# Selective scan in the last layer of a four-layer image network: which engine adds softplus' parts and multiplies by B, and where layer norm's PSUM tiles come from

## The chip, the cores and the metric

The kernel runs on one core of a Trainium2 chip. The time is the device time of one execution in microseconds (us). The core's engines are TensorE (PE, matmuls, with weight loads shown apart as PEld), VectorE (DVE), ScalarE (ACT), GpSimd (POOL), and SyncE (SP), which here issues nearly all transfers. Each engine works through its own queue in order; semaphores tie the queues together.

## The reference

Four layers follow each other on an image of 2 x 128 channels x 64 x 64: attention, a convolution block with deformable branches, three steps of a residual convolution, and a layer of selective scans. The change touches the last one alone. For each of two images it normalises over the channels, then runs the same scan block ("mamba") over the 4096 pixels in four orders (rows, rows backwards, columns, columns backwards), joins the four outputs by a linear layer and adds the input:

```python
xh, z = jnp.split(x @ W_in.T, 2, axis=-1)          # 256 channels each
xh = silu(causal_conv4(xh) + conv_b)
x_dbl = xh @ W_xp.T                                # 8 + 16 + 16 columns: dt, B, C
dt = softplus(x_dbl[..., :8] @ W_dt.T + b_dt)
dA = jnp.exp(dt[..., None] * -jnp.exp(A_log))      # decays, 256 x 16 states
dBu = dt[..., None] * Bm[:, :, None, :] * xh[..., None]
h = dA_t * h + dBu_t                               # over the pixels
y = jnp.einsum('lbdn,bln->bld', hs, Cm) + xh * Dp
return (y * silu(z)) @ W_out.T
```

## The kernel before

`layer3` cuts the work into 64 blocks: two images x four orders x eight stretches of 512 pixels (`BLK`). A block has 256 channels x 16 states = 4096 recurrences, which lie on 128 partitions as eight groups: two halves `hf` of the channels x four `ng` of the states. In a group, partition 32 j + c holds state 4 ng + j of channel c of a quarter, and the four quarters `q` lie beside each other: a tile `db` of 128 x 4 x 512. I call one of these 128 x 512 parts a state-column; a block has 32.

What is done for a group, and on which engine:

- `weights` (L1370, PE): a matmul with a selecting matrix spreads the four rows of B over the partitions, into the PSUM tile `pbc` (pool `psb`, two buffers).
- `db_dve` (L1386, DVE): `pbc` times dt x u for the first n of the four state-columns, n from the table `ND[hf][ng]`.
- `db_pool` (L1395, POOL): the other 4 - n state-columns, from a copy of B in SBUF. `copies` (L1380) brings these copies, and those of C, with four transfers each, for the groups that need them.
- `expo` (L1402, ACT): the decay of one state-column, into a PSUM tile `da` (pool `psd`, three buffers); it is issued two state-columns ahead.
- `scan` (L1411, DVE): the recurrence of one state-column, in place in `db`.
- `keep` (L1416, ACT): the last column of the four, for the next block.
- `cmul` (L1421, POOL): `db` times C for all four.
- `sums` (L1429, PE): four matmuls that sum over the states into `py` (one buffer); with the first `ng` also L1427, the product of u and D.
- `gate` (L1438, DVE): `py` times silu(z), once per half.

The tiles `db` come from a pool of four buffers, so a group's product waits for the sums of the group four before it.

What a block needs before its scans, its front, is spread over the eight turns of the loop (`slot`) of the block before: convolution (`begin`, `conv`, L1284), `conv_silu` (L1289), `xproj` and `xproj_copy` (L1308, L1314, L1316), `delta` (L1334), `softplus` (L1340 to L1343), `xproj_rest` (L1326, L1327) with `rest_copy` (L1330), which make the low part of B and C, `zproj` with `zproj_silu` (L1296, L1302), `spread` (L1348, L1349, POOL), and `spread_store`, `spread_load`, `bc_store` on SP, which lay dt and dt x u out on the partitions by way of DRAM. All front tiles in PSUM come from one pool, `psm`, with two buffers. Softplus is made from two parts, relu(v) in `dd[:, 0]` and ln(1 + exp(-|v|)) in `dd[:, 1]`.

What a block needs after its scans: `project` (L1446, L1448, PE: the image itself through an identity matrix, plus the output matmuls) and `finish` (L1454, L1456 or L1459, ACT), in slots 3 and 4 of the block after.

The layer norm of the first image runs ahead of the scans; that of the second (`ln_mean`, `ln_square`, `ln_var`, `ln_scale`, `ln_store`, L1211 to L1242) runs beside eight late blocks of the first image.

The order on every engine is the order in which the loop issues (`tc.manual_schedule`). A turn of the loop issues, in this order: transfers, `weights(k + 2)`, four times `expo` and `scan` with `keep(k - 1)` after the first expo, the products of group k + 1, `cmul(k - 1)`, the front's matmuls, the front's work on ACT and POOL, `project` or `finish`, the layer norm's step, and `sums(k - 2)`.

Of the kernel before, what the change touches and what calls it, by code (L numbers as in the profile page):

```python
# [20 lines left out]
P = 128  # L21
NB = 2
# [30 lines left out]
def interior(g, b, r0=0, rows=HW):  # L53
    return g.xa[:, b, 1 + r0 : 1 + r0 + rows, 1 : 1 + HW]
# [7 lines left out]
def img(t):  # L62
    return t.rearrange("p (r w) -> p r w", w=HW)
# [1057 lines left out]
def layer3(g, I, out):  # L1121
# [5 lines left out]
    nc, tc = g.nc, g.tc  # L1127
    NJ = 4

    ND = ((2, 4, 2, 4), (2, 4, 1, 4))  # L1130
    NNG = N_STATE // NJ
    HB = 1
    HC = 3
    with ExitStack() as ctx:
# [6 lines left out]

        winz = a.tile([P, 2, P], F32, name="winz")
        nc.sync.dma_start(winz, I["winzT"])
        wxp = a.tile([P, 2, 40], F32, name="wxp")
        nc.sync.dma_start(wxp, I["wxpT"])
        wdt = a.tile([40, 2, P], F32, name="wdt")
        nc.sync.dma_start(wdt[32:40], I["wdtT"])
        am = a.tile([P, 2, 4, NNG], F32, name="am")
        nc.sync.dma_start(am, I["alog4"])
        onesm = a.tile([P, P], F32, name="onesm")  # L1150
# [55 lines left out]
        N = {}  # L1206


        def ln_mean(b, k):
            N[k, "mean"] = psm.tile([P, BLK], F32, name="pm3")  # L1210
            nc.tensor.matmul(N[k, "mean"], onesm, interior(g, b, k * RB, RB), start=True, stop=True)  # L1211

        def ln_square(b, k):
            if b == 0:

                t = wk.tile([P, 4, BLK], F32, name="db")
                N[k, "xc"], N[k, "sq"] = t[:, 0, :], t[:, 1, :]
            else:
                N[k, "xc"] = ck.tile([P, BLK], F32, name="xc", bufs=1)
                N[k, "sq"] = ck.tile([P, BLK], F32, name="sq", bufs=1)  # L1220
            xc = N[k, "xc"]
            nc.vector.tensor_sub(img(xc), interior(g, b, k * RB, RB), img(N[k, "mean"]))  # L1222
            nc.scalar.activation(N[k, "sq"], xc, AF.Square)

        def ln_var(b, k):
            N[k, "var"] = psm.tile([P, BLK], F32, name="pm3")
            nc.tensor.matmul(N[k, "var"], onesm, N[k, "sq"], start=True, stop=True)

        def ln_scale(b, k):

            nc.scalar.activation(N[k, "sq"], N[k, "var"], AF.Ln, bias=g.eps5)
            nc.scalar.activation(N[k, "sq"], N[k, "sq"], AF.Exp, scale=-0.5)
            nc.gpsimd.tensor_mul(N[k, "xc"], N[k, "xc"], N[k, "sq"])

        def by_row(k):
# [69 lines left out]
        def xproj(i):  # L1305
            S[i]["px"] = px = psm.tile([P, BLK], F32, name="pm3")
            for hf in range(2):
                nc.tensor.matmul(px[:40, :], wxp[:, hf, :], S[i]["u"][:, hf, :], start=(hf == 0), stop=(hf == 1))  # L1308

        def xproj_copy(i):  # L1310

            px = S[i].pop("px")
            S[i]["xd"] = ck.tile([40, BLK], F32, name="xd", bufs=1)
            nc.scalar.copy(S[i]["xd"], px[:40, :])  # L1314
            bc = S[i]["bc"] = ck.tile([4 * N_STATE, BLK], F32R, name="bc")
            nc.scalar.copy(bc[0:32], px[0:32, :])  # L1316

# [13 lines left out]

        def delta(i, hf):
            pdt = S[i]["pdt", hf] = psm.tile([P, BLK], F32, name="pm3")
            nc.tensor.matmul(pdt, wdt[32:40, hf, :], S[i]["xd"][32:40], start=True, stop=True)  # L1334

        def softplus(i, hf):

# [4 lines left out]
            nc.scalar.activation(dd[:, 1, :], dd[:, 1, :], AF.Exp, scale=-1.0)  # L1342
            nc.scalar.activation(dd[:, 1, :], dd[:, 1, :], AF.Ln, bias=g.one)  # L1343

        def spread(i, hf):
            s_ = S[i]
            dd = s_["dd", hf]
            nc.gpsimd.tensor_add(dd[:, 0, :], dd[:, 0, :], dd[:, 1, :])  # L1348
            nc.gpsimd.tensor_mul(dd[:, 1, :], dd[:, 0, :], s_["u"][:, hf, :])  # L1349

        def spread_store(i, hf):
# [98 lines left out]
        def finish(i):  # L1450
            b, nd, c = blocks[i]
            s_ = S.pop(i)
            if nd == 0:
                nc.scalar.activation(s_["xv"], img(s_["pf"]), AF.Identity, bias=vec(g, "b_fuse"))  # L1454
            elif nd < 3:
                nc.scalar.copy(s_["xv"], img(s_["pf"]))  # L1456
            else:
                res = ck.tile([P, BLK], F32, name="sq", bufs=1)
                nc.scalar.copy(res, s_["pf"])  # L1459
                nc.sync.dma_start(out[b, :, c * BLK : (c + 1) * BLK], res)  # L1460

# [10 lines left out]
        def front_act(i, slot):  # L1472
            if i < NBK:
                if slot == 0:
                    conv_silu(i)
                elif slot == 1:
                    xproj_copy(i)
                elif slot == 2:
                    softplus(i, 0)
                elif slot == 3:  # L1480
                    softplus(i, 1)
                elif slot == 4:
                    rest_copy(i)
                elif slot == 5:
                    zproj_silu(i)


        def transfers(i, slot):
            if i < NBK:
                if slot == 2:  # L1490
                    bc_store(i)
                elif slot == 4:
                    spread_store(i, 0)
                elif slot == 5:
                    spread_load(i, 0)
                    spread_store(i, 1)
            if slot == 0 and i - 1 < NBK:
                spread_load(i - 1, 1)
            for x, ahead in (("b", 3), ("c", 1)):
                j, ng = divmod(8 * (i - 1) + slot + ahead, 8)  # L1500
                if ng < NNG and 0 < j < NBK:
                    copies(j, x, ng)

        def front_pe(i, slot):
            if i < NBK:
                if slot == 1:
                    xproj(i)
                elif slot == 2:
                    delta(i, 0)
                elif slot == 3:  # L1510
                    delta(i, 1)
                elif slot == 4:
                    xproj_rest(i)
                elif slot == 5:
                    zproj(i)
            if i + 1 < NBK:
                if slot == 6:
                    begin(i + 1)
                elif slot == 7:
                    conv(i + 1, 1)  # L1520

        def front_pool(i, slot):
# [1 line left out]
                if slot in (3, 4):  # L1524
                    spread(i, slot - 3)

        LN = {6: ln_mean, 7: ln_square, 8: ln_var, 9: ln_scale, 10: ln_store}

        def next_norm(i, slot):

            for j, s in ((i, slot), (i - 1, slot + 8)):
                b, k = divmod(j, 4 * NBLK)
                k -= 4 * NBLK - 2 - NBLK
                if j >= 0 and b + 1 < NB and 0 <= k < NBLK and s in LN:
                    LN[s](b + 1, k)

        with tc.manual_schedule():
            tc.keep_in_program_order(nc.scalar.preload_act_table_set("natural_log_exp_and_others"))
# [7 lines left out]
            for t in range(NBLK + 2):  # L1546
# [12 lines left out]
                elif slot in (3, 4):  # L1559
                    spread_store(0, slot - 3)  # L1560
                    if slot == 3:
                        spread_load(0, 0)
                        copies(0, "b", 0)
                        copies(0, "c", 0)
                for s in LN:
                    if 0 <= t - s // 8 < NBLK:
                        LN[s](0, t - s // 8)
                if t == 1:
                    begin(0)
                    conv(0, 1)  # L1570
            for ng in range(1, NNG):
                copies(0, "b", ng)
                copies(0, "c", ng)
            units = [(k, q) for k in range(len(groups)) for q in range(4)]
            AHEAD = 2
            for u in range(AHEAD):
                expo(*units[u])
            for k in range(len(groups) + 6):
                i, slot = divmod(k, 8)
                live = k < len(groups)  # L1580
                more = k + 1 < len(groups)
# [1 line left out]
                transfers(i + 1, slot)  # L1583
                if k + 2 < len(groups):
                    weights(k + 2)
                for q in range(4):
                    if 4 * k + q + AHEAD < len(units):
                        expo(*units[4 * k + q + AHEAD])
                    if q == 0 and ended:
                        keep(k - 1)  # L1590
                    if live:
                        scan(k, q)

                    for j, hf in (((k - 6) // 8, 0), ((k - 10) // 8, 1)):
                        if q == 1 and 8 * j + 6 + 4 * hf == k and 0 <= j < NBK:
                            gate(j, hf)
                if more:
                    db_dve(k + 1)
                    db_pool(k + 1)
                if ended:  # L1600
                    cmul(k - 1)
                front_pe(i + 1, slot)
                front_act(i + 1, slot)
                front_pool(i + 1, slot)
                if i >= 1 and i <= NBK:
                    if slot == 3:
                        project(i - 1)
                    elif slot == 4:
                        finish(i - 1)
                if live:  # L1610
                    next_norm(i, slot)

                    if slot == 6 and i % (4 * NBLK) < NBLK // 2:
                        for n in range(2):
                            turn(blocks[i][0], 2 * (i % (4 * NBLK)) + n)

                if 0 <= k - 2 < len(groups):
                    sums(k - 2)


# [86 lines left out]
def _arrays(i):  # L1707
# [26 lines left out]
    for d, (n, s) in enumerate((("offx", slice(0, 9)), ("offy", slice(9, 18)))):  # L1734
# [3 lines left out]
            for j, v in enumerate(("g", "b", "beta")):  # L1738
                offv[c, j] = l1[f"{n}_{v}"][s]
    wxp = l3["W_xp"]  # L1740
    wxp = np.concatenate([wxp[DTR:], wxp[:DTR]])
    a = {
        "x": i["x"].reshape(NB, P, L),
        "vecs": np.stack([cols[n] for n in VEC], axis=1),
# [5 lines left out]
        "w1T": taps(l2["w1"]), "w2T": taps(l2["w2"]),  # L1750
        "winX": l3["W_in"][: 2 * P].reshape(2, P, P).transpose(1, 0, 2),
        "winzT": l3["W_in"][2 * P :].reshape(2, P, P).transpose(2, 0, 1),
        "wxpT": wxp.reshape(40, 2, P).transpose(2, 1, 0),
        "wdtT": l3["W_dt"].reshape(2, P, DTR).transpose(2, 0, 1),

        "alog4": l3["A_log"].reshape(2, 4, 32, 4, 4).transpose(4, 2, 0, 1, 3).reshape(P, 2, 4, 4),
# [21 lines left out]
```

## Time and profile before

| | us |
|---|---|
| median of 3 runs | 5967.48 (5966.78 to 5974.58) |
| the profiled execution | 5965.63 |
| its span, first to last instruction | 5963.8 |
| first scan | 2517.65 after the span's start |
| DVE busy | 4521.3 (76%) |
| POOL busy | 3653.1 (61%) |
| ACT busy | 3768.4 (63%) |
| PE busy | 4905.1 (82%) |

The busy shares are means over four very different layers. The scans begin at 2517.65 us and fill the rest, some 3430 us. What bounds that stretch is read from windows within it. In a group of instructions, "busy" is the time covered by at least one of them; instructions of one engine overlap a little, so that a scan of 1265 ns comes every 1.18 us.

### The profile page before, as it was taken

The numbers are of one execution on the slowest core, as the hardware profiler recorded it, in microseconds if no ns is written. First come the engines' busy times: TensorE is split into PE (matmuls) and PEld (weight loads), VectorE is DVE, ScalarE is ACT, GpSimd is POOL, SyncE is SP. The second block draws the span as 40 slices with busy tenths as digits, with TensorE's granted clock in tenths as the row PEclk, the third lists the DMA queues.
The fourth block names the chain that finished last, engine by engine and source line by source line (L and its number), as shares of the span: only waits on it lengthen the run. The fifth ranks groups of instructions, "written<-read, shape, count | busy, mean of one in ns | idle before, by whom it ended". The sixth has DMA issues, their size and how long they took to land.

```text
span 5963.8 us, 57478 instructions
## 1 busy us (share of the span) xinstructions
PE 4905.1 (82%) x18726; PEld 1661.7 (28%) x18726; DVE 4521.3 (76%) x4266; ACT 3768.4 (63%) x5371; POOL 3653.1 (61%) x1328
## 2 busy tenths in 40 slices
PE   7999999989978689877777777777777777777776
PEld 3333333334444234222222222222222222222221
DVE  5333333364134688599999999999999999999998
ACT  4888888830035411477666766767776766767665
POOL 5111111100010121299999999999999999999998
PEclk8999999999989899877778777877788777877776
DMA  5000001030066100255555555554565555555554
GB/s 153 18 18 18 19 18 33 1 58 1 15 116 113 48 4 0 52 135 123 125 126 139 135 123 124 128 134 116 136 139 131 127 122 130 139 130 126 126 136 99
DMA packets 333092, 541.85 MB, mean 91 GB/s; under 512 B 66504, under 2 KB 121168, under 8 KB 331696
## 3 DMA queue, kind: packets, MB, share of 16 engines
q1 hardware_dynamic: 329648, 534.54, 39.0%
q10 hardware_dynamic: 3136, 3.56, 0.2%
q8 instruction: 149, 2.44, 0.2%
q14 instruction: 159, 1.30, 0.1%
HBM read 448.78 MB, written 89.13 MB: 90 GB/s over the span
## 4 chain that ended last, share of the span: by engine, by line
PE 39%; DVE 37%; ACT 6%; issue 6%; DMA 6%; POOL 4%; SPq 1%; DVEq 0%; POOLq 0%; ACTq 0%
DVE db L1411 25%; PE ps L287 10%; DVE db L1386 10%; PE acc L303 8%; PE m L1052 5%; PE m L566 5%; DMA dx<-dd 3%; POOL db L1421 2%; ACT da L1402 2%; PE acd L812 2%; PE pm L1296 1%; PE m L526 1%; ACT L1303 1%; ACT L1302 1%; PE pf L775 1%
## 5 line engine op out<-in xcount | busy, mean ns | idle before, releaser
L1421 POOL TENSOR_TENSOR db<-db,c 128x2048 f32<-128x2048 f32 x512 | 2310.7, 4528 | 21.6 <-ACT hl L1416 21.1
L1411 DVE TENSOR_TENSOR_SCAN db<-da,hl,db 128x512 f32<-128x512 f32 x1792 | 2165.0, 1265 | 61.3 <-ACT da L1402 14.9
L1402 ACT ACTIVATE da<-dd,am 128x512 f32<-128x512 f32 x2048 | 1403.5, 689 | 963.3 <-DVE db L1411 953.7
L293 ACT ACTIVATE e<-ps 128x1024 f16<-128x1024 f32 x1024 | 992.2, 1021 | 134.7 <-PE ps L287 117.5
L1386 DVE TENSOR_TENSOR db<-pbc,dd 128x2048 f32<-128x2048 f32 (+2 forms) x512 | 851.8, 1664 | 19.8 <-PE py L1429 18.2
L1370 PE MATMUL pbc<-bc,sel 64*128 64x512 f32 x512 | 288.5, 564 | 571.7 <-DVE db L1386 571.4
L1395 POOL TENSOR_TENSOR db<-b,dd 128x1024 f32<-128x1024 f32 (+1 forms) x256 | 671.6, 2623 | 119.9 <-issue 94.5
L1429 PE MATMUL py<-db,fold 128*32 128x512 f32 x4096 | 640.5, 703 | 104.8 <-POOL db L1421 104.7
L314 DVE RECIPROCAL rec<-acc 32x512 f32<-32x512 f32 x64 | 214.9, 3358 | 639.2 <-PE acc L303 612.1
L321 POOL TENSOR_TENSOR parts<-parts 32x512 f32<-32x512 f32 x64 | 80.4, 1256 | 975.3 <-DVE parts L320 975.3
L287 PE MATMUL ps<-q,k 32*128 32x512 f32 x4096 | 656.2, 643 | 3.5 <-DVE flag L250 2.7
L303 PE MATMUL acc<-e,v 128*128 128x512 f16 x2048 | 531.3, 382 | 0.0
L1052 PE MATMUL m<-v,u 128*128 128x512 f32 x864 | 377.2, 600 | 51.0 <-DVE v L1021 51.0
L1370 PEld LDWEIGHTS pbc<-bc,sel 64*128 64x128 f32 x512 | 106.2, 208 | 1113.4 <-DVE db L1386 1048.3
L1284 PE MATMUL pm<-xn,wcs 128*128 128x512 f32 x512 | 285.0, 708 | 56.9 <-DVE xc L1222 46.3
L1411 DVE TENSOR_TENSOR_SCAN db<-da,db 128x512 f32<-128x512 f32 x256 | 294.4, 1205 | 17.4 <-ACT da L1402 8.7
L303 PEld LDWEIGHTS <-v 128*128 128x128 bf16 x2048 | 158.5, 97 | 509.8 <-issue 388.5
L287 PEld LDWEIGHTS ps<-q,k 32*128 32x128 f32 x4096 | 229.7, 183 | 227.9 <-issue 147.1
L1284 PE MATMUL pm<-xt,wcs 128*128 128x512 f32 x512 | 279.2, 696 | 11.3 <-ACT z L1302 11.3
L1427 PE MATMUL py<-u,ddp 128*128 128x512 f32 x256 | 186.4, 818 | 101.7 <-DVE gt L1438 101.7
L566 PE MATMUL m<-comb,w 64*128 64x512 f32 (+4 forms) x1296 | 269.9, 575 | 0.0
L686 POOL TENSOR_SCALAR yt<-y 32x512 f32<-32x512 f32 x8 | 18.2, 2270 | 381.2 <-DVE y L677 380.8
(315 smaller groups left out, 5970.5 us busy)
## 6 DMA issues: line engine op xcount, KB each, us to landing
dd<-dx SPq DMA_DIRECT2D x1024, 256.0 KB, 6.6
dx<-dd SPq DMA_DIRECT2D x128, 512.0 KB, 8.7
c<-bx SPq DMA_DIRECT2D x1024, 64.0 KB, 2.3
hats<-pos SPq DMA_DIRECT2D x136, 256.0 KB, 9.6
b<-bx SPq DMA_DIRECT2D x512, 64.0 KB, 5.2
q<-qd SPq DMA_DIRECT2D x32, 512.0 KB, 8.6
w<-in_conv0T SPq DMA_DIRECT2D x18, 288.0 KB, 8.5
q<-in_x SPq DMA_DIRECT2D x8, 512.0 KB, 7.6
```

The costliest lines, as they stand in the source:

```text
L287: nc.tensor.matmul(ps[:, i, :], k4[h % 2][rows, kb // 4, :], q4[h % 2][rows, qb * BLK : (qb + 1) * BLK], start=True, stop=True,)
L293: nc.scalar.activation(e[:, :n, :], ps[:, :n, :], AF.Exp)
L303: nc.tensor.matmul(acc, v3[b][:, kb, h, :], e[:, i, :], start=(kb == 0), stop=(kb == NS - 1))
L566: yield lambda q=q, dy=dy, src=src, i0=i0, i1=i1: nc.tensor.matmul(m[:, i0 * NF : i1 * NF], w[half, dy, q, x, :], src, start=(dy == KC and ...
L1052: nc.tensor.matmul(m[x], weights[j][:, dy, x, :], v[j][b][:, x, r0 : r0 + RP, :].rearrange("p r i -> p (r i)"), start=(dy == 0), stop=(dy ...
L1284: nc.tensor.matmul(pu, wcs[:, hf, s, :], window(blk, sgn * s), start=(s == 0), stop=(s == 3))
L1386: nc.vector.tensor_tensor(x["db"][:, :n, :], x.pop("pb").unsqueeze(1).to_broadcast([P, n, BLK]), S[i]["d4", hf][:, 1, :n, :], ALU.mult)
L1395: nc.gpsimd.tensor_tensor(x["db"][:, n:, :], S[i]["b", ng].unsqueeze(1).to_broadcast([P, 4 - n, BLK]), S[i]["d4", hf][:, 1, n:, :], ALU.mult)
L1402: nc.scalar.activation(da, S[i]["d4", hf][:, 0, q, :], AF.Exp, scale=am[:, hf, q, ng : ng + 1])
L1411: nc.vector.tensor_tensor_scan(d1, d0, d1, 0.0 if first else hl[:, hf, ng, q, :], ALU.mult, ALU.add)
L1421: nc.gpsimd.tensor_mul(v, v, S[i]["c", ng].unsqueeze(1).to_broadcast([P, 4, BLK]))
L1429: nc.tensor.matmul(S[i]["y", hf][32 * q : 32 * q + 32, :], fold, G[k]["db"][:, q, :], start=False, stop=(ng == NNG - 1),)
```

## The change

- **Products with B.** The table `ND` gives DVE 21 of a block's 32 state-columns where it had 23, and POOL 11 where it had 9, in other groups; three of the four `ng` need a copy of B in SBUF instead of two.
- **Softplus.** The two parts are added by PE: `sum_parts` multiplies both by the identity into one PSUM tile of `psm`, and `sum_copy` (ACT) writes the sum over `dd[:, 0]`. `spread` on POOL loses its addition.
- **dt.** W_xp gets a second copy of its dt rows at row 64, so that each half's `delta` reads its own eight rows; both halves' matmuls are issued in slot 1.
- **The front's slots.** The front moves one slot ahead, with `conv_silu` at the end of slot 7 of the block before; `project` goes from slot 3 to slot 5, after the sums of that slot, and `finish` from slot 4 to the head of slot 6.
- **Layer norm.** Its two PSUM tiles come from the pool of the decays. Its steps for the second image are placed by hand in slots 0, 1, 3, 4 and 6.
- `finish` has a tile of its own, `res`, for the last order's result.

The diff, cut to its core:

```diff
-    ND = ((2, 4, 2, 4), (2, 4, 1, 4))
+    ND = ((4, 2, 1, 4), (1, 4, 1, 4))
...
-        wxp = a.tile([P, 2, 40], F32, name="wxp")
+        wxp = a.tile([P, 2, 72], F32, name="wxp")
...
+        def ln_tile():
+            return psd.tile([P, BLK], F32, name="da")
         def ln_mean(b, k):
-            N[k, "mean"] = psm.tile([P, BLK], F32, name="pm3")
+            N[k, "mean"] = ln_tile()
...
         def delta(i, hf):
             pdt = S[i]["pdt", hf] = psm.tile([P, BLK], F32, name="pm3")
-            nc.tensor.matmul(pdt, wdt[32:40, hf, :], S[i]["xd"][32:40], start=True, stop=True)
+            r = slice(32 + 32 * hf, 40 + 32 * hf)
+            nc.tensor.matmul(pdt, wdt[r], S[i]["xd"][r], start=True, stop=True)
...
+        def sum_parts(i, hf):
+            ps = S[i]["dt", hf] = psm.tile([P, BLK], F32, name="pm3")
+            for x in range(2):
+                nc.tensor.matmul(ps, g.ident, S[i]["dd", hf][:, x, :], start=(x == 0), stop=(x == 1))
+        def sum_copy(i, hf):
+            nc.scalar.copy(S[i]["dd", hf][:, 0, :], S[i].pop(("dt", hf)))
         def spread(i, hf):
             s_ = S[i]
             dd = s_["dd", hf]
-            nc.gpsimd.tensor_add(dd[:, 0, :], dd[:, 0, :], dd[:, 1, :])
             nc.gpsimd.tensor_mul(dd[:, 1, :], dd[:, 0, :], s_["u"][:, hf, :])
...
         def front_act(i, slot):
             if i < NBK:
                 if slot == 0:
-                    conv_silu(i)
+                    xproj_copy(i)
                 elif slot == 1:
-                    xproj_copy(i)
+                    softplus(i, 0)
                 elif slot == 2:
-                    softplus(i, 0)
+                    softplus(i, 1)
+                    sum_copy(i, 0)
                 elif slot == 3:
-                    softplus(i, 1)
+                    sum_copy(i, 1)
+                    rest_copy(i)
                 elif slot == 4:
-                    rest_copy(i)
-                elif slot == 5:
                     zproj_silu(i)
+            if i + 1 < NBK and slot == 7:
+                conv_silu(i + 1)
...
         def front_pe(i, slot):
             if i < NBK:
-                if slot == 1:
+                if slot == 0:
                     xproj(i)
+                elif slot == 1:
+                    delta(i, 0)
+                    delta(i, 1)
                 elif slot == 2:
-                    delta(i, 0)
+                    sum_parts(i, 0)
                 elif slot == 3:
-                    delta(i, 1)
+                    sum_parts(i, 1)
+                    xproj_rest(i)
                 elif slot == 4:
-                    xproj_rest(i)
-                elif slot == 5:
                     zproj(i)
             if i + 1 < NBK:
-                if slot == 6:
+                if slot == 5:
                     begin(i + 1)
-                elif slot == 7:
+                elif slot == 6:
                     conv(i + 1, 1)
...
                 if k + 2 < len(groups):
                     weights(k + 2)
+                norm = next_norm(i)
+                if slot == 6 and 1 <= i <= NBK:
+                    finish(i - 1)
                 for q in range(4):
+                    if norm and slot == 3 and q == 3:
+                        ln_log(*norm)
                     if 4 * k + q + AHEAD < len(units):
                         expo(*units[4 * k + q + AHEAD])
+                    if norm and q == 0:
+                        if slot == 0:
+                            ln_mean(*norm)
+                        elif slot == 3:
+                            ln_var(*norm)
...
+                if norm and slot == 0:
+                    ln_less(*norm)
                 if more:
                     db_dve(k + 1)
                     db_pool(k + 1)
                 if ended:
                     cmul(k - 1)
+                if slot == 5 and 0 <= k - 2 < len(groups):
+                    sums(k - 2)
+                if slot == 5 and 1 <= i <= NBK:
+                    project(i - 1)
                 front_pe(i + 1, slot)
                 front_act(i + 1, slot)
                 front_pool(i + 1, slot)
-                if i >= 1 and i <= NBK:
-                    if slot == 3:
-                        project(i - 1)
+                if norm:
+                    if slot == 1:
+                        ln_square(*norm)
+                    elif slot == 3:
+                        ln_root(*norm)
                     elif slot == 4:
-                        finish(i - 1)
+                        ln_scale(*norm)
+                    elif slot == 6:
+                        ln_store(*norm)
...
-                if 0 <= k - 2 < len(groups):
+                if slot != 5 and 0 <= k - 2 < len(groups):
                     sums(k - 2)
```

`bc_store` moves from slot 2 to slot 1. Ahead of the loop, the first image's layer norm goes through the same new functions, and `conv_silu` of block 0 follows its convolution.

## The prediction

> **What bounds the kernel now.** I read the stages first, then the waits, then one block in order of time. The stretch from the first to the last scan lasts 3430 us of the span. Its columns are length, busy time (instructions) of PE, PEld, DVE, ACT and POOL, clock, DMA share, GB/s:
>
> ```profile
> core 0: us, PE busy (x) PEld busy (x) DVE busy (x) ACT busy (x) POOL busy (x), PEclk, DMA share, GB/s
> 2600.00:5900.00 3300.00, 2506.45 (x7100) 703.49 (x7098) 3213.14 (x2592) 2306.03 (x3732) 3165.05 (x993) 0.79 0.56 130
> ```
>
> DVE is busy 97.4% and POOL 95.9%: two engines near their end, so the waits decide. All that DVE waits for there is some 36 us; POOL waits three times as much:
>
> ```profile
> POOL db L1395 <- issue: 90.2, 53, 3.4
> ...
> DVE db L1386 <- PE py L1429: 18.2, 8, 2.9
> ...
> DVE db L1411 <- ACT da L1402: 15.6, 58, 0.5
> ```
>
> So DVE sets the pace. I number the eight groups of a block, and the loop's turns (slots), 0 to 7; T3 is the start of slot 3's first scan. DVE's timeline, from slot 3's scans to slot 7's:
>
> ```profile
> 3336.61 4.81 DVE L1411 TENSOR_TENSOR_SCAN db<-da,hl,db 128x512 f32<-128x512 f32 x4
> 3341.34 1.20 DVE L1386 TENSOR_TENSOR db<-pbc,dd 128x1024 f32<-128x1024 f32 x1
> 3342.64 4.81 DVE L1411 TENSOR_TENSOR_SCAN db<-da,hl,db 128x512 f32<-128x512 f32 x4
> 3347.36 2.26 DVE L1386 TENSOR_TENSOR db<-pbc,dd 128x2048 f32<-128x2048 f32 x1
> 3349.73 4.81 DVE L1411 TENSOR_TENSOR_SCAN db<-da,hl,db 128x512 f32<-128x512 f32 x4
> 3354.45 0.67 DVE L1386 TENSOR_TENSOR db<-pbc,dd 128x512 f32<-128x512 f32 x1
> 3355.22 2.46 DVE L1411 TENSOR_TENSOR_SCAN db<-da,hl,db 128x512 f32<-128x512 f32 x2
> 3357.60 0.67 DVE L1438 TENSOR_TENSOR gt<-py,z 128x512 f32<-128x512 f32 x1
> 3358.52 2.46 DVE L1411 TENSOR_TENSOR_SCAN db<-da,hl,db 128x512 f32<-128x512 f32 x2 [0.26 <-ACT da L1402]
> 3360.90 2.27 DVE L1386 TENSOR_TENSOR db<-pbc,dd 128x2048 f32<-128x2048 f32 x1
> 3363.27 4.81 DVE L1411 TENSOR_TENSOR_SCAN db<-da,hl,db 128x512 f32<-128x512 f32 x4
> ```
>
> From start to start, a slot lasts 6.03 us if the product at its end is two state-columns wide, 7.09 if four, 5.49 if one. A gate adds 0.59. Slot 6 lasts 8.05, not 7.68: DVE waits for a decay, 0.26 us plus lost overlap (0.35). A block is 4 x 7.09 + 3 x 6.03 + 5.49 + 2 x 0.59 + 0.35 = 53.5 us, with no room left.
>
> **What the Trainium skill says.** "GPSIMD Engine Reference", 3.1: a two-input operation on 2048 fp32 takes 4497 ns on GpSimd and 2293 on VectorE; here 4528 (L1421) and 2264 (L1386). Its section 1 says that the two share SBUF interfaces, with contention when VectorE has two SBUF inputs; here L1421 takes 4.49 to 4.56 us beside scans and products alike, each of which reads one input from PSUM. "PSUM — Partial Sum Buffer", Specifications: GpSimd has no access to PSUM, so a product moved there needs B in SBUF. "TensorE: Matmul & The Clock Gate", Part 1: the array runs at half rate until a window of about 3.4 us was busy. Agreed, and sharper: in 3.41 us intervals the clock (after the busy time) is 0.50 or 1.00.
>
> ```profile
> 3378.78:3382.19 3.41, 3.41 (x10) 0.50 0.10 22
> 3382.19:3385.61 3.42, 2.31 (x9) 1.00 0.24 78
> 3385.61:3389.02 3.41, 2.57 (x9) 0.50 0.00 0
> ...
> 3392.43:3395.85 3.42, 3.42 (x5) 0.50 0.00 0
> 3395.85:3399.26 3.41, 3.41 (x15) 1.00 0.19 76
> ```
>
> Over all such intervals from 2700 to 5900 us, at half clock about 2.65 us of matmuls bring the full clock next, and at full clock about 1.4 us keep it; the 8-row L1334 and the 64-row L1370 don't count.
>
> **The change, part by part.**
>
> *Products.* Widths on DVE by group go from 2,4,2,4,2,4,1,4 to 4,2,1,4,1,4,1,4: 21 state-columns for 23. A block of slots is then 4 x 7.09 + 6.03 + 3 x 5.49 + 2 x 0.59 = 52.04. Against 53.13 without the wait, DVE gains 1.09 us by these rounded steps; the rows' means give 2 x (1197 - 663) = 1.07. I take 1.05, and x 64 blocks **-67 us**.
>
> *POOL.* Rows:
>
> ```profile
> L1395 POOL TENSOR_TENSOR db<-b,dd 128x1024 f32<-128x1024 f32 x192 | 451.6, 2352 | 119.9 <-issue 94.5 <-DMA c<-bx 14.3 <-POOL db L1421 4.5
> ...
> L1395 POOL TENSOR_TENSOR db<-b,dd 128x1536 f32<-128x1536 f32 x64 | 220.0, 3437 | 0.0
> ...
> L1348 POOL TENSOR_TENSOR dd<-dd 128x512 f32<-128x512 f32 x128 | 162.2, 1267 | 0.0
> ```
>
> Three two-wide and one three-wide product (10.5) become one and three (12.7); both adds L1348 go (-2.5); eight L1421 (36.1) and two L1349 (2.5) stay. 51.7 becomes 51.3, starts overlapping a little: about 51.1, inside DVE's 52.0. About 1 us per block is left for waits. Now POOL loses 1.7 us a time to the sums of group 0 (90.2/53; L1395 starts at 3336.12, L1429 ended at 3335.96). After it, sum_parts stands ahead of those sums on PE; they end 6.6 to 8.3 us after T2 (below), POOL arrives at about 7.3. A wait of at most 1 us, 0.3 on average: covered.
>
> *DMA.* One more copy of B, four 64 KB transfers a block on SP (b and c copies took 8.7 us for eight at 3353). Chain: end of POOL's spread, store 2.7, loads 3.8, store 0.6, eight copies 8.7, landing 5.2 (median) = 21 us; POOL has 22.7 us of work before it needs group 1's copy. Cost 0, margin 1.6. bc_store moves ahead of c's third copy, which is needed two slots later: 0.
>
> *Softplus.* Per half two fp32 matmuls (four rows: 2.0 us at full clock, 4.0 at half, from L1446 and L1448) and one ACT copy (0.58). PE gains 4 us of 52 at full clock, ACT 1.2.
>
> *ScalarE's slots.* An expo needs a free da tile, so in each slot ACT starts its other work 4.38 us after T (3349.73 to 3354.11) and the next expo is ready 0.72 after that work; DVE wants it at the next T + 2.38, or 2.97 with a gate. Check: now slot 5 has zproj's 3.68, 4.38 + 3.68 + 0.72 = 8.78 against 5.49 + 2.97 = 8.46: the measured wait. After: slot 0 6.2 against 8.4; slot 1 (softplus 2.42) 7.5 against 8.5; slot 2 (softplus, copy, gate) 8.7 against 10.1; slot 3 (two copies) 6.3 against 7.9; slot 4 (zproj) 8.8 against 9.5; slot 7 (conv_silu 3.88) 9.0 against 9.5. All fit; today's 0.35 goes.
>
> *What is late next.* Slot 5 has no front work, but slot 6 opens with finish (1.15 on ACT), which waits for project. On PE slot 5 is L1370 0.45, sums 1.03, project 2.9, then conv 3.7: project ends 4.4 us after T5 at full clock, 8.5 at half. ACT needs it by 8.46 - 0.72 - 1.15 = 6.6. PE idles 3 us before T5, so it mostly starts or drops into half clock; with the interval rule project ends near 6.1 for two thirds of the phases and at 7.1 to 7.6 for the others: 0.2 us a block. Behind it on PE stand conv and the sums of group 4, wanted 11 us later.
> Slots 2 and 3: L1370 and sum_parts start at T2 + 1.3 (softplus' end) at half clock, with ddp and sums 8 us of full-height matmuls. That brings the full clock between 4.0 and 7.4 us after T2, so they end at 6.6 to 8.3, and slot 3 (0.45 + 2.0 + 2.3 of xproj_rest) ends 4.8 to 5.4 after T3. rest_copy wants it at 5.0 and has 1.6 us in hand: 0.
> Waits: 0.35 - 0.2 = 0.15 x 64 = **-10 us**.
>
> *Layer norm.* Today the eight blocks that carry it last 21 us longer in sum (18.2 of it the wait for L1429, eight times: mean and var take psm tiles ahead of zproj and conv). After, the tiles are decays' tiles: an expo may wait for ln_less, covered by a product and two scans. There remain 0.6 (DVE's subtraction) and about 1 us in slot 3 (var ahead of sum_parts, two ACT steps more), 13 us: **-8 us**. The start (first scan at 2517.65) gains free psm tiles and loses conv_silu of block 1, now ahead of the first expo (3.9): 0, between -8 and +6. The tail after the last scan keeps its chain.
>
> Sum: -67 - 10 - 8 = -85; I take -83. The profiled execution took 5965.63, its span 5963.8; the median is 1.9 higher: 5967.5 - 83 = **5885**.
>
> **The rivals.**
> *The gain is half lost to ACT or POOL.* Project late in every block by 1 us, or POOL adding its present 1.7 us to 51.1: 52.8 to 53.1 per block, -0.4 to -0.7, 5915 to 5940. For it: project at half clock is 8.5. Against: most phases turn to full clock in time.
> *Slower: PE at half clock through slots 2 and 3.* If matmuls against the identity don't lift the clock (L1446, the only like row, always runs beside L1448; with 1.85 of it and 1.56 of L1448 the clock rose, with L1334's it didn't), slot 2 ends 1.5 after T3, xproj_rest at 10.7, the expo is ready at 12.0 against 7.9: 4.1 us. At the present share of half-clock intervals there (6 in 10) that is 2.5 a block: 52.04 + 2.7 - 53.5 = +1.25, x 64 = +80, less 8: **6040**. It decides once the mean wait passes 1.4 us a block.
> *It doesn't do what it says:* excluded for widths and matmuls, which stand in the instruction order.
>
> **Numbers.** Forecast 0.65 (5852 to 5910), half lost 0.22, slower 0.10, nothing left 0.03. Range 5852 to 5942. A measurement here tells 0.2% (12 us) from no change: faster 0.87, same 0.03, slower 0.10.
>
> **What would show it.** DVE slots of 5.49 after groups 1, 3 and 5; block period 52.0 to 52.6; L1348 gone and POOL's idle near 1 us a block; no DVE wait for decays in slots 1 to 5 and 7, a small one in slot 6; no wait of L1386 for sums in the layer-norm blocks. I am wrong if DVE idles over 0.5 us a block for ACT, if xproj_rest ends over 6.6 us after T3, or if POOL stands behind a B copy.

## The result, and the profile after

The changed kernel takes **5899.3 us** (median of four runs, 5897.97 to 5905.25) against 5968.2 for the kernel before, run beside it: a ratio of 0.9884, with a 95% interval of 0.9867 to 0.9902. Its profiled execution took 5899.89 us (span 5898.1), 65.7 fewer than the 5965.63 of before. The forecast was 5885, the range 5852 to 5942. The kernel before, run beside each of the experiments below, has medians of 5967.1 to 5970.6, and in the profiles the three earlier layers, which no edit touches, end between 2450.6 and 2460.0 us: a difference of some 3 us between two medians tells nothing here.

The stage of the scans, in the same columns as before (the last scan now ends at 5883 us, so the stretch stops at 5830):

```profile
core 0: us, PE busy (x) PEld busy (x) DVE busy (x) ACT busy (x) POOL busy (x), PEclk, DMA share, GB/s
2600.00:5830.00 3230.00, 2526.33 (x7579) 772.17 (x7578) 3143.30 (x2588) 2348.40 (x3849) 3141.01 (x870) 0.84 0.58 138
```

DVE is busy 97.3% and POOL 97.2%: the two are now equally near their end. A POOL block is 0.972 x 52.54 (the mean block) = 51.1 us, the figure of the prediction. The clock granted rose from 0.79 to 0.84. The waits of the same stretch (us in total, times, longest):

```profile
ACT xa L1474 <- PE pm L1466: 85.1, 32, 4.9
...
POOL db L1439 <- ACT hl L1434: 71.6, 55, 2.2
...
ACT xa L1472 <- PE pm L1466: 46.4, 16, 5.0
...
DVE db L1429 <- ACT da L1420: 33.1, 29, 3.2
...
ACT res L1477 <- PE pm L1466: 31.8, 13, 4.8
```

Two of before's lines are gone: DVE's 18.2 us behind the sums in the layer-norm blocks, and POOL's 90.2 us before L1395. POOL's idle time now stands mostly behind ScalarE's keep (L1434), 1.3 us a time, and DVE waits for POOL's products 0.6 us in all. New are 163 us in which ScalarE waits for project (85.1 + 46.4 + 31.8): finish needs L1466. ScalarE has room; what counts is the 33.1 us that DVE waits for decays (15.1 in the same stretch before). The runs below divide them between project and the layer norm. DVE in order of time, from slot 5's scans to slot 7's product in block 12:

```profile
3180.66 4.81 DVE L1429 TENSOR_TENSOR_SCAN db<-da,hl,db 128x512 f32<-128x512 f32 x4
3185.38 0.67 DVE L1404 TENSOR_TENSOR db<-pbc,dd 128x512 f32<-128x512 f32 x1
3186.16 2.46 DVE L1429 TENSOR_TENSOR_SCAN db<-da,hl,db 128x512 f32<-128x512 f32 x2
3188.53 0.67 DVE L1456 TENSOR_TENSOR gt<-py,z 128x512 f32<-128x512 f32 x1
3189.11 2.45 DVE L1429 TENSOR_TENSOR_SCAN db<-da,hl,db 128x512 f32<-128x512 f32 x2
3191.48 2.27 DVE L1404 TENSOR_TENSOR db<-pbc,dd 128x2048 f32<-128x2048 f32 x1
3193.85 4.81 DVE L1429 TENSOR_TENSOR_SCAN db<-da,hl,db 128x512 f32<-128x512 f32 x4
3198.57 2.27 DVE L1404 TENSOR_TENSOR db<-pbc,dd 128x2048 f32<-128x2048 f32 x1
```

Slot 5 now ends with a one-wide product: 5.50 us from 3180.66 to 3186.16. Slot 6 is 7.69 here (3186.16 to 3193.85) and not 8.05: behind the gate DVE doesn't wait. So it is in half of the blocks, and their period is 52.08 us, in place of 53.485; in the others slot 6 lasts up to 2.8 us longer.

To account for the rest I summed, slot by slot over all 64 blocks, what each slot lasts beyond its usual length (scan starts from the trace; the first block of a direction, whose scans are 0.06 us shorter, against its own length):

| us beyond the usual slot | before | after |
|---|---|---|
| slot 0, in the eight turns with a layer norm | 18.9 | 4.8 |
| slot 4, the same | 0.0 | 14.7 |
| slot 7, the same | 3.3 | 0.0 |
| slot 6, all blocks | 24.0 | 24.7 |
| anywhere else | 0.5 | 0.4 |

The usual block went from 53.13 to 52.08, x 64 = -67.2, and another -1.1 because the first block's product of group 0, now two columns wider, lies ahead of the first scan. With the -2.1 of the table the stretch between the first and the last scan is 70.4 us shorter. The first scan starts 5.7 later (2523.34 for 2517.65), and the tail is 1.1 shorter: -65.8, which is the measured 65.7 but for rounding.

### The profile page after: what moved, and what is told of

Read it like the earlier page. It is cut to its first block, busy times and chain, and to the rows that moved or that the text cites. A ratio compares the mean times of both kernels' runs of the same rounds, so it can differ in the third digit from the quotient of the medians.

```text
span 5898.1 us, 58825 instructions
## 1 busy us (share of the span) xinstructions
PE 4930.2 (84%) x19238; PEld 1735.4 (29%) x19238; DVE 4452.2 (75%) x4266; ACT 3816.1 (65%) x5499; POOL 3632.0 (62%) x1200
## 3 DMA queue, kind: packets, MB, share of 16 engines
q8 instruction: 152, 2.49, 0.2%
## 4 chain that ended last, share of the span: by engine, by line
PE 52%; DVE 27%; POOL 9%; issue 5%; DMA 4%; ACT 2%; SPq 1%; DVEq 0%; POOLq 0%; ACTq 0%
DVE db L1429 18%; PE ps L287 10%; PE acc L303 8%; DVE db L1404 7%; POOL db L1439 6%; PE pm L1294 6%; PE m L1052 6%; PE m L566 5%; PE py L1447 2%; PE pm L1359 2%; PE pm L1466 2%; PE pm L1464 2%; PE acd L812 2%; DMA dx<-dd 1%; POOL dd L1367 1%
## 5 line engine op out<-in xcount | busy, mean ns | idle before, releaser
L1388 PE MATMUL pbc<-bc,sel 64*128 64x512 f32 x512 | 288.3, 563 | 695.4 <-DVE db L1404 695.3
L1413 POOL TENSOR_TENSOR db<-b,dd 128x1536 f32<-128x1536 f32 (+1 forms) x256 | 811.5, 3170 | 9.0 <-PE py L1447 4.4
L1404 DVE TENSOR_TENSOR db<-pbc,dd 128x2048 f32<-128x2048 f32 (+2 forms) x512 | 785.3, 1534 | 0.6 <-PE pbc L1388 0.6
L1388 PEld LDWEIGHTS pbc<-bc,sel 64*128 64x128 f32 x512 | 105.8, 207 | 1184.1 <-DVE db L1404 1070.4
L1359 PE MATMUL pm<-dd,ident 128*128 128x512 f32 x512 | 365.3, 852 | 4.6 <-ACT dd L1352 4.4
L686 POOL TENSOR_SCALAR yt<-y 32x512 f32<-32x512 f32 x8 | 18.2, 2272 | 379.8 <-DVE y L677 379.4
L1052 PEld LDWEIGHTS m<-v,u 128*128 128x128 f32 x864 | 166.9, 194 | 262.1 <-issue 216.1
L1294 PE MATMUL pm<-xn,wcs 128*128 128x512 f32 x512 | 237.1, 606 | 3.0 <-ACT z L1312 2.6
```

The costliest lines, as they stand in the source:

```text
L1052: nc.tensor.matmul(m[x], weights[j][:, dy, x, :], v[j][b][:, x, r0 : r0 + RP, :].rearrange("p r i -> p (r i)"), start=(dy == 0), stop=(dy ...
L1294: nc.tensor.matmul(pu, wcs[:, hf, s, :], window(blk, sgn * s), start=(s == 0), stop=(s == 3))
L1404: nc.vector.tensor_tensor(x["db"][:, :n, :], x.pop("pb").unsqueeze(1).to_broadcast([P, n, BLK]), S[i]["d4", hf][:, 1, :n, :], ALU.mult)
L1413: nc.gpsimd.tensor_tensor(x["db"][:, n:, :], S[i]["b", ng].unsqueeze(1).to_broadcast([P, 4 - n, BLK]), S[i]["d4", hf][:, 1, n:, :], ALU.mult)
```

## The experiments

All times stand against the 5899.3 us of the kernel after unless said otherwise.

**The products alone.** The kernel before with one line of the change:

```diff
-    ND = ((2, 4, 2, 4), (2, 4, 1, 4))
+    ND = ((4, 2, 1, 4), (1, 4, 1, 4))
```

> The kernel before with the new table ND alone; softplus' additions stay on GpSimd, the front keeps its slots. Theory (GpSimd's room for the two state-columns comes from the two additions): GpSimd needs 8 x 4.51 + 2.35 + 3 x 3.40 + 2 x 2.55 = 53.7 us a block, over VectorE's 52.0, so the block lasts 53.7 us or more: 5980 to 6060 us, VectorE idle 1.5 us a block and more, waiting for sums or for GpSimd's products. Rival (VectorE's work alone sets the pace): 1.05 x 64 = 67 us less than before, 5901 to 5935 us with some new waits for decays.

Measured: 6048.4 us (6047.57 to 6049.06), 1.0131 times before (1.0114 to 1.0148): slower by 1.3%. Its stage and its waits:

```profile
2600.00:5830.00 3230.00, 2452.66 (x6793) 688.17 (x6795) 3012.14 (x2472) 2197.08 (x3565) 3146.94 (x950) 0.77 0.57 132
```

```profile
DVE db L1411 <- POOL db L1395: 119.1, 74, 5.3
```

DVE falls to 93.3% while POOL stays at 97.4%, and DVE waits for POOL's products (L1395), which it did not do before. The narrower groups are a loss unless something else leaves POOL.

**The additions back on POOL.** The kernel after with the sum of softplus' parts on GpSimd again (no sum_parts, no sum_copy):

```diff
         def spread(i, hf):
...
+            nc.gpsimd.tensor_add(dd[:, 0, :], dd[:, 0, :], dd[:, 1, :])
             nc.gpsimd.tensor_mul(dd[:, 1, :], dd[:, 0, :], s_["u"][:, hf, :])
```

> The changed kernel with both of softplus' additions on GpSimd again, and neither sum_parts nor sum_copy. Theory (GpSimd has about 1 us a block to spare, no more): its work becomes 51.1 + 2.6 = 53.7 us, the block about 53.7 to 54.2: 5975 to 6010 us, with VectorE waiting some 1.5 us a block. Rival (GpSimd isn't near its bound, its busy time only follows VectorE): 5890 to 5905 us, the four matmuls and two copies less being worth nothing or a little.

Measured: 5994.2 us (5991.33 to 5996.33), 95 more than the kernel after and 1.0037 times before (1.0023 to 1.0051).

```profile
2600.00:5830.00 3230.00, 2371.22 (x6916) 666.29 (x6915) 3060.29 (x2516) 2227.23 (x3627) 3200.55 (x965) 0.77 0.57 134
```

POOL is at 99.1%, a block lasts 54.0 us on average, and DVE waits for POOL again (101.0 us in 59 waits).

**One of the two additions back.** As above, for half 1 only.

> The kernel after with only half 1's addition of softplus' parts put back on GpSimd (half 0's stays on TensorE and ScalarE). Theory (GpSimd has a slack per block, and work costs nothing until it is used up): busy time of GpSimd in the kernel after is 3141 of 3230 us, 50.65 us of each 52.08 us block; one addition more is 51.9 us, and at the 99.1% that it reached with both additions a block lasts 52.4 us: 64 x 0.3 = some 20 us over the kernel after, 5905 to 5935 us. Rival (each addition costs its share whatever the slack): half of the 95 us that both cost, about 5947 us.

Measured: 5906.1 us (5902.32 to 5907.18), 7 more.

```profile
2600.00:5830.00 3230.00, 2488.83 (x7323) 741.23 (x7324) 3142.30 (x2585) 2314.81 (x3786) 3210.04 (x931) 0.82 0.58 138
```

The first addition costs 7 us, the second 88, for the same work: the first fills POOL's slack (97.2% to 99.4%), the second has none left. A cost in proportion (5947) is ruled out. The 7 us are a net figure. Slot 6 is 39.4 us too long over all blocks, for 24.7 in the kernel after, while slot 4 of the layer-norm blocks has 6.4 us too much, for 14.7: in the slot ahead of it sum_parts and sum_copy are gone. With both additions slot 6 has 131.8 us too much. So the first costs about 15 us in slot 6 and the second 92. An estimate from the 1.0 us of slack that the prediction gave POOL, and 1.27 us for an addition, is 0.27 x 64 = 17 and 1.27 x 64 = 81.

**All but the products.** The kernel after with 23 state-columns on DVE:

```diff
-    ND = ((4, 2, 1, 4), (1, 4, 1, 4))
+    ND = ((4, 4, 1, 4), (1, 4, 1, 4))
```

> The changed kernel with two state-columns given back to VectorE (widths 4,4,1,4,1,4,1,4: 23 on VectorE as before, 9 on GpSimd). Theory (the gain is the two state-columns, at 0.53 us each per block): 5899 + 1.06 x 64 = 5967 us, within 8 us, and the wait in slot 6 unchanged at some 0.36 us a block. Rival (the gain comes from the additions on TensorE, the earlier front or the layer norm's tiles): 5899 to 5920 us.

Measured: 5956.0 us (5949.78 to 5961.79): 56.7 more than after, 3 us under the theory's range. The usual block is 53.14 us for 52.08, so the columns are worth 68 us, as costed. But slot 6 lasts only 12.2 us too long over all blocks, not 24.7, and gives some of it back. Why is seen in the waits:

```profile
POOL db L1439 <- ACT hl L1434: 226.1, 108, 4.6
```

POOL, with less work and a longer block, waits 226 us (71.6 in the kernel after) for keep, which follows DVE's scans, and no longer lags behind them. In the first blocks of a direction slot 6 has 3.2 us too much, for 12.8. So a part of the slot 6 wait comes from POOL.

**Project at the end of slot 4.** What waits in slot 6 is finish, for project. PE in slot 5, first in a usual block (44, slot 5 starts at 4873.65), then in the first block of a direction (16, at 3388.94), both of the kernel after:

```profile
4874.46 1.29 PE L1447 MATMUL py<-db,fold 128*32 128x512 f32 x8 [0.38 <-POOL db L1439]
4875.69 2.27 PE L1464 MATMUL pm<-xa,ident 128*128 128x512 f32 x2
4877.77 2.28 PE L1466 MATMUL pm<-gt,mt 128*128 128x512 f32 x4
```

```profile
3391.00 1.94 PE L1447 MATMUL py<-db,fold 128*32 128x512 f32 x8 [1.61 <-POOL db L1439]
3392.86 2.26 PE L1464 MATMUL pm<-xa,ident 128*128 128x512 f32 x2
3394.95 2.99 PE L1466 MATMUL pm<-gt,mt 128*128 128x512 f32 x4
```

In the first, project ends 6.4 us after the slot's start. In the second the sums ahead of it wait 1.61 us for POOL's products with C, and project ends at 9.0. Over all blocks the ends average 6.8 in the 56 usual ones and 8.3 in the seven first blocks with a project (block 0 has none): their scans are shorter, POOL's work is not, and POOL falls behind. The later start of the sums (1.85 us after T5 on average, for 0.78) is 1.1 of these 1.5 us. The granted clock adds to it: from T5 to the end of project it was 0.62 in block 16 and 0.73 in block 44. The edit takes project out from behind those sums:

```diff
-                if slot == 5 and 1 <= i <= NBK:
-                    project(i - 1)
...
                 if slot != 5 and 0 <= k - 2 < len(groups):
                     sums(k - 2)
+                if slot == 4 and 1 <= i <= NBK:
+                    project(i - 1)
```

> The changed kernel with project at the end of slot 4, where TensorE idles 3 us, instead of slot 5. Theory (the wait of VectorE in slot 6 is finish waiting for project at half clock): project ends by about 3 us after slot 5 begins at the latest, the wait of 0.36 us a block goes, 23 us less: 5872 to 5882 us. Rival (something else holds the decays in slot 6, or project there delays group 3's sums and with them gate): 5895 us or more.

Measured: **5878.6 us** (5876.16 to 5883.11), 20.7 fewer. Slot 6 is 2.7 us too long over all blocks, for 24.7 (in the first blocks 2.4, for 12.8); project ends 3.7 us after T5 on average. DVE's wait for decays is down to the layer-norm blocks:

```profile
DVE db L1429 <- ACT da L1420: 12.2, 8, 3.2
```

**The layer norm's place in the order.** The kernel after with ln_var behind the other work of slot 3:

```diff
-                    if norm and slot == 3 and q == 3:
+                    if norm and slot == 4 and q == 2:
                         ln_log(*norm)
...
-                        elif slot == 3:
-                            ln_var(*norm)
...
                     elif slot == 3:
-                        ln_root(*norm)
+                        ln_var(*norm)
                     elif slot == 4:
+                        ln_root(*norm)
+                    elif slot == 5:
                         ln_scale(*norm)
```

> The kernel after with the second layer norm's variance matmul issued behind the other TensorE work of slot 3 and not ahead of it, its Ln in slot 4, its rsqrt's Exp at the end of slot 4, its last product on GpSimd in slot 5. Theory (slot 4 of six of the eight blocks with a layer norm is 2.05 to 3.3 us long because sum_parts and rest_copy stand behind the variance matmul, and the decays behind those on ScalarE): the excess goes, 8 to 15 us: 5884 to 5892 us. Rival (the decays are late because a layer-norm tile takes one of their three PSUM tiles, wherever it is held): the same excess appears in slot 4 or 5, 5895 to 5905 us.

Measured: 5888.6 us (5882.4 to 5890.39), 10.7 fewer. Slot 4's 14.7 us are gone; slot 5 now has 4.2 us too much, some 0.5 in each of the eight blocks: the rival's effect, small.

**The layer norm's tiles.** The kernel after, in its order, with the second layer norm's two tiles taken from the front's pool again:

```diff
-        def ln_tile():
-            return psd.tile([P, BLK], F32, name="da")
+        def ln_tile(b):
+            if b:
+                return psm.tile([P, BLK], F32, name="pm3")
+            return psd.tile([P, BLK], F32, name="da")
```

> The kernel after with the second layer norm's two PSUM tiles taken from the front's pool (pm, two tiles) as before and not from the decays' (da, three tiles); the order of the work is the changed one. Theory (in the decays' rotation the variance matmul waits up to 1.2 us for a scan to free its tile, and what stands behind it on TensorE waits with it; a pm tile has been free since slot 2): 5 to 10 us fewer than the kernel after, 5889 to 5895 us. Rival (the place in the order sets the loss and not the pool): within the scatter of the kernel after, 5897 to 5905 us. Other rival (two pm tiles are too few once layer norm shares them): over 5908 us.

Measured: **5882.8 us** (5880.41 to 5888.21), 16.5 fewer, more than the theory gave. Slot 4 has 2.2 us too much in all, for 14.7; that is 12.5 of the 16.5. From the first scan to the last the profile is 14.1 us shorter, and the rest lies within the scatter of the four runs (8 us). Block 23, slot 3 (its scans start at 3747.45 after and at 3747.71 here). First PE and ACT of the kernel after:

```profile
3747.40 0.49 PE L1388 MATMUL pbc<-bc,sel 64*128 64x512 f32 x1 [2.37 <-DVE db L1404]
3748.78 2.07 PE L1233 MATMUL da<-sq,onesm 128*128 128x512 f32 x2 [0.89 <-DVE db L1429]
```

```profile
3749.94 0.69 ACT L1420 ACTIVATE da<-dd,am 128x512 f32<-128x512 f32 x1 [1.59 <-DVE db L1429]
3751.12 0.69 ACT L1420 ACTIVATE da<-dd,am 128x512 f32<-128x512 f32 x1 [0.48 <-DVE db L1429]
...
3755.51 0.57 ACT L1340 CAST bc<-pm 32x512 fp32r<-32x512 f32 x1 [1.59 <-PE pm L1337]
3756.11 0.63 ACT L1240 ACTIVATE sq<-sq 128x512 f32<-128x512 f32 x1
3756.65 0.67 ACT L1420 ACTIVATE da<-dd,am 128x512 f32<-128x512 f32 x1
```

and the same with the tile from pm:

```profile
3748.09 1.13 PE L1234 MATMUL pm<-sq,onesm 128*128 128x512 f32 x2
```

```profile
3749.03 0.69 ACT L1421 ACTIVATE da<-dd,am 128x512 f32<-128x512 f32 x1 [0.42 <-DVE db L1430]
3750.21 0.69 ACT L1421 ACTIVATE da<-dd,am 128x512 f32<-128x512 f32 x1 [0.48 <-DVE db L1430]
...
3753.84 0.57 ACT L1341 CAST bc<-pm 32x512 fp32r<-32x512 f32 x1 [1.24 <-PE pm L1338]
3754.44 0.63 ACT L1241 ACTIVATE sq<-sq 128x512 f32<-128x512 f32 x1
3754.98 0.68 ACT L1421 ACTIVATE da<-dd,am 128x512 f32<-128x512 f32 x1
```

In the decays' rotation of three, the variance tile does two things at once. Its matmul waits for a scan (0.89 us), and what is behind it on PE, down to rest_copy, with it. And with one tile lent out, a decay can start only when the scan two before it is done and not three: the second decay of the slot starts 2.49 us after the scans' start, against 1.32. A third thing follows. PE, which waits, has little work in the interval ahead of the variance matmul, and the clock granted in the next interval is half. PE's busy time, its clock, the DMA share and GB/s, in the kernel after and then with the tile from pm:

```profile
3745.36:3748.77 3.41, 0.49 (x1) 1.00 0.00 0
3748.77:3752.19 3.42, 3.40 (x4) 0.50 0.02 5
```

```profile
3744.28:3747.69 3.41, 1.68 (x11) 1.00 0.00 0
3747.69:3751.10 3.41, 3.24 (x7) 1.00 0.00 0
```

Together the decay behind rest_copy starts 9.20 us after the scans' start and not 7.27, and DVE, which wants it at once, waits:

```profile
3757.35 2.46 DVE L1429 TENSOR_TENSOR_SCAN db<-da,hl,db 128x512 f32<-128x512 f32 x2 [1.95 <-ACT da L1420]
```

Most of the loss goes with the clock. In six of the eight layer-norm blocks of the kernel after it falls to half within slot 3; there rest_copy starts 8.0 to 9.3 us after T3, and slot 4 is 2.05 to 3.3 us too long. In the other two, with the same wait and the same lent tile, the clock stays full, rest_copy starts at 6.4, and slot 4 is 0.4 us too long. With the tile from pm one block of eight falls to half clock (1.1 us too long); six of the others have 0.13 us. Eight blocks tell these shares only roughly, but in the last run below, again with pm, it is one of eight too.

**The start.** The kernel after with block 1's conv_silu moved from ahead of the first decays into slot 0 of the first block.

```diff
+                if k == 0:
+                    conv_silu(1)
                 front_pe(i + 1, slot)
...
-            if i + 1 < NBK and slot == 7:
+            if i > 0 and i + 1 < NBK and slot == 7:
                 conv_silu(i + 1)
```

> The kernel after with block 1's conv_silu taken from the end of the stretch before the loop into the first slot, behind that slot's decays. Theory (the 5.7 us by which the first scan starts later than before are 3.85 us of Silu and table loads ahead of the first decays, and a later layer-norm chain): the first scan starts 3.8 us earlier, at about 2519.5 us of the profile, and 2 to 4 us are kept in the time: 5895 to 5898 us. Rival (the 3.85 us are only moved: ScalarE has no room for them in the first slots): no gain, 5898 to 5902 us.

Measured: 5896.6 us (5895.42 to 5898.82). The number falls to the theory, the profile to the rival:

```profile
2519.27 4.57 DVE L1429 TENSOR_TENSOR_SCAN db<-da,db 128x512 f32<-128x512 f32 x4 [6.52 <-ACT da L1420]
...
2530.96 2.34 DVE L1429 TENSOR_TENSOR_SCAN db<-da,db 128x512 f32<-128x512 f32 x2 [3.57 <-ACT da L1420]
```

The first scan starts 4.07 us earlier, but in slot 1 DVE waits 3.57 us for decays, and block 1 starts at 2572.91 for 2573.20. ScalarE has no room for the Silu and its table loads there. The 2.7 us between the medians are not that saving, as the next runs show.

**Together.** Project in slot 4, the later ln_var and the moved conv_silu:

> The last two edits together with the projection issued at the end of slot 4. If the three stalls are apart from one another their gains add: 5878.6 less 8 to 15 for the layer norm and 2 to 4 for the start, 5860 to 5869 us. If one stall only covered another, it stays above 5872 us.

Measured: 5866.7 us (5864.16 to 5870.46): 20.7 + 10.7 off 5899.3 is 5867.9, so the two stalls are apart. Without the moved conv_silu:

> The project step at the end of slot 4 and the later variance matmul together, without the move of block 1's conv_silu. Theory (that move only shifts 3.6 of its 4.1 us into slot 1 of the first block): the same as with all three within 1.5 us, 5865 to 5869 us. Rival (it is worth the 2.7 us between the medians of its own run and the kernel after): 5869 to 5872 us.

Measured: 5866.8 us (5860.95 to 5870.15). The move is worth nothing that can be told within a scatter of 6 and 9 us. Last, project in slot 4 with the layer norm's tiles in pm:

> The kernel after with the second layer norm's two tiles in the front's pool pm and the project step at the end of slot 4: the two edits that gained most by themselves. Theory (two separate stalls): 5899.3 less 20.7 for the projection and 16.5 for the pool is 5862 us; the sum of the slots gives 6.9 us of layer norm where the version with the later variance matmul kept 8.9, so 5862 to 5867 us. Rival (with the projection's tile in slot 4 the pool's two tiles are too few in the blocks with a layer norm): over 5870 us.

Measured: **5863.2 us** (5861.86 to 5865.52), 0.9827 times before (0.9813 to 0.984), inside the theory's 5862 to 5867. Against the kernel before beside them the last two stood at 0.9830 and 0.9826, so the three are level, and this one needs two small edits.

```profile
2600.00:5830.00 3230.00, 2529.38 (x7632) 763.50 (x7632) 3173.22 (x2615) 2370.75 (x3875) 3172.91 (x877) 0.85 0.58 139
```

DVE and POOL are at 98.2% each. Of stalls, 7.0 us of layer norm (4.8 of them its own subtraction on DVE) and 4.0 of slot 6 remain.

## Why the prediction was right, and where it was off

*Products, -67:* right. The usual block shrank by 1.05 us, and putting the two columns back costs 68 in block lengths.

*POOL, no cost and 1 us of slack:* right. It is the reason why the change works: without the additions' move the same widths cost 1.3%, and the slack is what one addition (15 us in slot 6) and two (107) measure from both sides.

*Softplus on PE and ACT, no cost:* right. The DVE slots 1 to 3 are at their usual length. The slower rival needed matmuls against the identity that don't lift the clock, and they do. Three quarters of the way through slot 2 PE is at full clock in 50 of the 64 blocks; in the run with both additions back on POOL, without sum_parts, in none. In the first of these two intervals of the kernel after (PE busy, clock, DMA share, GB/s) sum_parts keeps PE busy throughout, beside 0.04 us of L1388:

```profile
3475.71:3479.12 3.41, 3.41 (x5) 0.50 0.02 6
3479.12:3482.53 3.41, 2.09 (x11) 1.00 0.00 0
```

The Trainium skill ("TensorE: Matmul & The Clock Gate", Part 1) states full rate after a busy window of about 3.4 us; the trace agrees for these.

*Waits, -10:* wrong; measured +0.7 (24.0 to 24.7). The old wait (zproj ahead of the decays) is gone from slot 6, as said, though no run undid the front's move by one slot, or the second dt rows, alone. In the 56 usual blocks the new one is about 0.2 us, as said: 24.7 less 12.8 is 11.9. The step that failed is project's start. "On PE slot 5 is L1370 0.45, sums 1.03, project 2.9" takes the sums as ready; in six of the seven first blocks with a project they wait 1.3 to 1.6 us for POOL. Slot 6 of the first blocks is 12.8 us too long in sum, 10.4 of which go when project moves. I had costed POOL's lag for its own queue and not for who reads its products.

*Layer norm, -8:* right in sign, wrong in size; measured -2.7 (slots 0, 4 and 7: 22.2 to 19.5). The old 18.2 us behind the sums did go, and DVE's 0.6 in slot 0 came as said. What was under-sized is "about 1 us in slot 3", 8 us over eight blocks: it cost 14.7 us, in slot 4. I had looked at the first tile's effect on the decays (ln_less, covered) and not at the second's, in a slot with no room, and had PE at full clock in slot 3, where it fell to half in six of the eight. At full clock the loss was 0.4 us a block. With the tiles from pm, 12.5 of the 14.7 us go.

*Start, 0 between -8 and +6:* +5.7, the upper end. From the end of the earlier layers to the first scan it is 5.2 (70.1 for 64.9); the other 0.5 lies in those layers, within their scatter. 3.9 is conv_silu, which I saw and set against a gain from freer tiles that didn't come: the last ln_store there starts 1.7 us later (2517.93 for 2516.22), and not earlier. Moved into slot 0, conv_silu costs DVE 3.6 us of waiting in slot 1.

In sum -68.3 + 0.7 - 2.7 - 0.1 + 5.7 - 1.1 = -65.8, where -83 was forecast (its terms give -85). The number held because the products, by far the largest term, were right; the waits, the layer norm and the start all came out worse, and none made up for another.

Two of the three signs of being wrong came nevertheless. DVE idles 33.1 us for ACT's decays in 61.5 blocks, 0.54 us a block where 0.5 was the limit. And xproj_rest ends 8.0 to 9.2 us after T3 in six layer-norm blocks, where 6.6 was. They point at the two terms above, waits and layer norm. The third hardly came: POOL's products waited three times, 3.0 us in all, and by the profile for copies of C.

## What to carry to other kernels

When two engines both stand near 97%, work moved to one pays only if at least as much leaves it, and its slack per period tells at which addition the cost starts: the first cost 0.2 us a block, the second its full length. A buffer borrowed from a rotation that feeds the bottleneck costs twice, once for the borrower, which queues for it, and once for the rotation, which is one shorter while it is lent. Here the price was 0.4 us a block, and 2 to 3 us where the borrower's wait came with a fall of PE's clock. For a step that is moved on an engine with a fixed order, cost what stands ahead of it there, and who that waits for: here two lines of order were worth 21 us.

## What the runs showed of the hardware that I had not expected

The engine that is second in line shows up in a third one's queue. In the first block of a direction DVE is faster by 0.06 us a scan (1.20 for 1.26; these scans read no `hl`), so that POOL lags; PE then waits 1.61 us for POOL's products, ScalarE for PE, and DVE for ScalarE: the 0.25 us that a slot gains comes back as a wait of 0.2 to 2.8 us in slot 6. And a short wait of PE can cost more than its length: behind the variance matmul's 0.9 us, rest_copy starts 6.4 us after T3 where the clock stayed full and 8.0 to 9.3 where it fell.
